# Layer 2's last layer norm in each pair of items applied in the scan layout, and one item's last statistics moved to ScalarE

## The chip, the cores and the metric

The kernel runs on one core of a Trainium2 chip. The metric is the device time of one execution in microseconds (us); lower is better. A core has TensorE (PE, with its weight loads shown as PEld), VectorE (DVE), ScalarE (ACT), GpSimd (POOL) and SyncE (SP, which here only issues DMAs). Each engine works through its own list of instructions in order, and waits for the others by semaphores.

## What is computed

The reference, cut to what matters here (the feed-forward part that follows is not touched by the change):

```python
def _mingru(x, Wz, bz, Wh, bh):
    z = sigmoid(einsum('bsi,hi->bsh', x, Wz) + bz)
    h_tilde = tanh(einsum('bsi,hi->bsh', x, Wh) + bh)
    a = clip(1.0 - z, CLAMP_LO, CLAMP_HI)
    return _linear_scan(a, z * h_tilde)              # along the sequence

def _stack(x, Wz, bz, Wh, bh, gamma, beta):          # 4 layers
    h = x
    for i in range(4):
        h_new = _mingru(h, Wz[i], bz[i], Wh[i], bh[i])
        if i > 0:
            h_new = h_new + h
        h = _layernorm(h_new, gamma, beta)
    return h

h_fwd = _stack(layernorm(x), ...)
h_bwd = flip(_stack(flip(layernorm(x)), ...))
x = x + einsum(concat(h_fwd, h_bwd), fusion_W) + fusion_b
x = x + ffn(layernorm(x))                            # 512 -> 2048 -> 512
```

x is 8 x 512 x 512 in float32 (batch, sequence, features). Both directions use the same weights, and the gates' two weight matrices are the same one, so one product per gate serves sigmoid and tanh.

## The kernel before, in words

**Layout.** Products and scans work with features on the 128 partitions and the sequence along the free axis: a state `h` is 4 chunks (`NC_`) of 128 x 512. The scan runs along the free axis. A layer norm is over the features, that is over partitions and chunks, so PE turns the state first: one group of 4 transposes (L316, in `turned`) gives `pt`, 128 positions by all 512 features, in PSUM.

**A layer norm between layers (`norm`).** For each of 4 row tiles: turn (L316); DVE makes mean and variance (`stats`, L171 to L182); POOL makes the inverse root `rs` (L178); ACT writes the normalised row tile `tok` (`normalise`, L188 and L189). When all four are there, 4 groups of 4 transposes (L325, in `back`) turn them back into `pf`, and ACT writes chunk c of `h` with gamma as scale and beta as bias (L331). Tiles `pt` have 2 PSUM banks (`ps_t`), tiles `pf`, `pr`, `py` share 2 (`ps_f`), the products' `u` have 4 (`ps_u`).

**After the last layer (`norm_last`)** only the statistics are made: turn, `stats` with no shift, and `rs` into a column of `rsv`. The mean is folded into the fusion weights; `rsv` is the scale of the fusion's products (L609).

**Order.** The kernel takes the 8 batch items in 4 pairs. Within a pair there are four streams, called items s = (b,0), (b,1), (b+1,0), (b+1,1) (batch, direction). First layer 0 for both batches, then layers 1, 2, 3, in each the four streams one after the other, each with 4 gate products (`layer`, `gates`). So layer 3 of a pair has 16 products. Then the fusion of both batches, mixed with layer 0 of the next pair.

The order in which instructions are issued is written out by `slot`. A slot issues one unit of work (a product of 4 matmuls and its three ACT activations), then what the queues have ready: `turns` and `backs` (norms), `xturns` and `xbacks` (statistics of the next pair's x, of which `scale_x` turns the scales into `pr`; in the last pair, the tokens of the feed-forward part, `py`). Then come the DVE's end of the unit (clamp L485, product L490, scan L494), then delayed stages of kind "resid", then the ACT part of what was taken from the queues. So on ACT, what a slot turned is drained after that slot's three activations:

```python
last = shares(cap) + x_shares()
due("scans")
if end is not None:
    end()
due("resid")
for f in last:
    if f is not None:
        f()
now[0] += 1
```

In layer 3 the residual sums h + z (L571) of a stream are "resid" stages, chunk c in slot 3 + c counted from the stream's first slot; its turns (`norm_last`) start in slot `now + NC_ + 1`, so that the turns of stream (b,1) come with the first slot of (b+1,1), the thirteenth of the layer. While streams (b+1,0) and (b+1,1) run, the statistics of the next pair's x are made too (L171, `st_x`).

The norm of layer 2's last stream (b+1,1) falls into the first slots of layer 3; its result is needed in the thirteenth.

## Time and profile before

| | |
|---|---|
| median of 3 runs | 1713.87 us (1713.86 to 1713.90) |
| the profiled execution's own time | 1714.24 us |
| its span, first to last instruction | 1712.0 us |
| granted TensorE clock | 1.00 |
| gate products (L462), 1536 matmul instructions | 593 ns mean of one, pipelined |
| turn for a norm (L316), 128 x 128 | 1024 transposes, 273 ns mean, pipelined |
| turn back (L325), 128 x 128 | 768 transposes, 273 ns mean, pipelined |
| scan (L494), 128 x 512 | 256, 1.23 to 1.24 us |
| DVE statistics of a turned tile (L171) | 256, 693 ns |
| DVE sum of two 128 x 512 (L571, L565) | 665 to 693 ns |
| ACT affine from PSUM (L331) | 192, 786 ns |

The span is cut by the profile into PE, DVE, ACT and POOL busy times. A matmul's duration in the profile includes its way through the pipeline, so that the mean of one is longer than the distance between two starts. Idle time before an instruction is given with the engine and line that ended it.

### The profile page before, as it was taken

To read this page: it belongs to the slowest core of one execution; us is meant where nothing else is said; L and a number is where in the kernel's file an instruction comes from. 1 tells how busy PE (TensorE), PEld (TensorE's weight loads), DVE (VectorE), ACT (ScalarE), POOL (GpSimd) and SP (SyncE) were. 2 spreads that over 40 slices of the span, in tenths; PEclk is the share of its full clock that TensorE was granted. 3 is DMA by queue.
4 is the path that set the end of the run, shared out by engine and by line. 5 is a ranking of instruction groups with operands and counts; after the bars stand their busy time and mean duration, and the time that the engine had idled before them with its cause. 6 is when DMAs were issued, how large, how long until landed. Compare 5 with 4: busy or idle time off the path is not lost.

```text
span 1712.0 us, 19766 instructions
## 1 busy us (share of the span) xinstructions
PE 1701.1 (99%) x6440; PEld 1042.4 (61%) x6440; DVE 1453.2 (85%) x2859; ACT 1074.6 (63%) x1858; POOL 222.3 (13%) x342
## 2 busy tenths in 40 slices
PE   9999999999999999999999999999999999999999
PEld 5455554555555455555545555554688888888887
DVE  7999989889998998999899899996568768768877
ACT  5898873468886246888524688860366566666654
POOL 3111111111111111111111111110000000000000
PEclk9999999999999999999999999999999999999999
DMA  8002231150000125000012200202201101100100
GB/s 271 19 25 81 99 93 37 65 193 1 1 19 13 56 68 191 1 1 19 13 56 69 104 21 29 74 1 99 74 1 50 50 0 50 49 19 31 50 19 31
DMA packets 46598, 91.74 MB, mean 54 GB/s; under 512 B 5280, under 2 KB 5536, under 8 KB 45472
## 3 DMA queue, kind: packets, MB, share of 16 engines
q1 hardware_dynamic: 45488, 88.78, 15.3%
q10 hardware_dynamic: 1008, 1.70, 0.3%
q8 instruction: 51, 0.84, 0.2%
q14 instruction: 51, 0.42, 0.1%
HBM read 65.30 MB, written 25.17 MB: 53 GB/s over the span
## 4 chain that ended last, share of the span: by engine, by line
PE 79%; DVE 16%; ACT 2%; issue 1%; DMA 1%; POOL 0%; DVEq 0%; ACTq 0%
PE u L462 28%; PE po L909 14%; PE ph L882 14%; PE pu L599 10%; PE pt L316 5%; DVE z L494 4%; PE pf L325 4%; PE u L511 4%; DVE st L171 2%; DVE z L490 2%; DVE a L485 1%; DVE z L565 1%; DVE zf L494 1%; PE py L214 1%; DVE mv L173 1%
## 5 line engine op out<-in xcount | busy, mean ns | idle before, releaser
L462 PE MATMUL u<-xT,gw 128*128 128x512 f32 x768 | 345.5, 593 | 0.0
L462 PE MATMUL u<-h,gw 128*128 128x512 f32 x768 | 345.5, 592 | 0.0
L494 DVE TENSOR_TENSOR_SCAN z<-a,z 128x512 f32<-128x512 f32 x224 | 274.9, 1227 | 7.6
L462 PEld LDWEIGHTS u<-xT,gw 128*128 128x128 f32 x768 | 138.6, 190 | 138.7 <-issue 136.8
L462 PEld LDWEIGHTS u<-h,gw 128*128 128x128 f32 x768 | 138.6, 190 | 138.2 <-issue 138.0
L479 ACT ACTIVATE a<-u,ngb 128x512 f32<-128x512 f32 x192 | 131.6, 685 | 139.6 <-PE u L462 139.1
L178 POOL TENSOR_TENSOR rs<-ve,mhalf 128x1 f32<-128x1 f32 x192 | 122.3, 637 | 679.8 <-DVE nmu L182 663.2
L171 DVE BATCH_NORM_STATS2 st<-pt 128x6 f32<-128x512 f32 x256 | 177.3, 693 | 37.7 <-PE pt L316 37.3
L909 PE MATMUL po<-pwq,ghi 128*128 128x512 f32 x512 | 202.7, 396 | 0.0
L882 PE MATMUL ph<-yhi,fcq 128*128 128x512 f32 x512 | 199.7, 390 | 0.0
L909 PE MATMUL po<-pwq,glo 128*128 128x512 f32 x512 | 199.6, 390 | 0.0
L882 PE MATMUL ph<-ylo,fcq 128*128 128x512 f32 x512 | 199.4, 389 | 0.0
L886 ACT ACTIVATE g<-ph 128x512 f32<-128x512 f32 x128 | 76.4, 597 | 186.2 <-PE ph L882 186.2
L490 DVE TENSOR_TENSOR z<-z,t 128x512 f32<-128x512 f32 x224 | 153.5, 685 | 10.3 <-ACT z L481 10.1
L189 ACT ACTIVATE tok<-pt,nmr,rs 128x512 f32<-128x512 f32 x192 | 149.3, 778 | 6.4
L897 DVE TENSOR_TENSOR acc<-acc,g 128x512 f32<-128x512 f32 x112 | 77.3, 691 | 84.7 <-ACT g L886 83.8
L481 ACT ACTIVATE z<-u,gb 128x512 f32<-128x512 f32 x192 | 132.4, 689 | 0.0
L480 ACT ACTIVATE t<-u,gb 128x512 f32<-128x512 f32 x192 | 130.8, 681 | 0.0
L316 PEld LDWEIGHTS pt<-ident,z 128*128 128x128 f32 x640 | 78.8, 141 | 77.4 <-issue 47.7
L511 PE MATMUL u<-xT,gw 128*128 128x512 f32 x256 | 115.0, 593 | 1.2 <-DVE gw L744 0.8
L599 PE MATMUL pu<-fw,xT 128*128 128x512 f32 x256 | 115.2, 593 | 0.0
L599 PE MATMUL pu<-fw,h 128*128 128x512 f32 x256 | 115.1, 592 | 0.0
(158 smaller groups left out, 2569.2 us busy)
## 6 DMA issues: line engine op xcount, KB each, us to landing
xf<-in_x_dram SPq DMA_DIRECT2D x32, 256.0 KB, 5.6
x<-xf SPq DMA_DIRECT2D x32, 256.0 KB, 2.0
xy<-x SPq DMA_DIRECT2D x32, 256.0 KB, 4.2
xn<-in_x_dram SPq DMA_DIRECT2D x31, 256.0 KB, 4.5
out_dram<-xy SPq DMA_DIRECT2D x31, 256.0 KB, 2.0
xT<-in_xt_dram SPq DMA_DIRECT2D x7, 1024.0 KB, 7.4
fca<-in_fc_wT_dram SPq DMA_DIRECT2D x16, 256.0 KB, 3.0
pwa<-in_proj_wT_dram SPq DMA_DIRECT2D x16, 256.0 KB, 2.6
```

Source lines behind the costliest of these rows:

```text
L171: nc.vector.bn_stats(st, src)
L189: nc.scalar.activation(dst, src, AF.Identity, bias=nmr, scale=rs)
L316: nc.tensor.transpose(pt[:, ts(c, P)], zs[c][:, ts(t, P)], ident)
L462: nc.tensor.matmul(u, lhsT=gw[l][:, c, ts(o, P)], rhs=h[:, c, :], start=(c == 0), stop=(c == NC_ - 1),)
L479: nc.scalar.activation(a, u, AF.Sigmoid, bias=ngb[:, l, o : o + 1], scale=-1.0)
L481: nc.scalar.activation(z, u, AF.Sigmoid, bias=gb[:, l, o : o + 1])
L490: nc.vector.tensor_tensor(z, z, t, ALU.mult)
L494: nc.vector.tensor_tensor_scan(dst[:, d], a[:, d], z[:, d], 0.0, ALU.mult, ALU.add)
L511: nc.tensor.matmul(u, lhsT=gw[0][:, c, ts(o, P)], rhs=xT[b][:, c, :], start=(c == 0), stop=(c == NC_ - 1),)
L599: nc.tensor.matmul(pu, lhsT=hs[d][:, c, ts(t, P)], rhs=fw[:, d * NC_ + c, :], start=(c == 0), stop=(c == NC_ - 1),)
L882: nc.tensor.matmul(ph, lhsT=w, rhs=ys[b][c][i], start=(c == 0 and i == 0), stop=(c == NC_ - 1 and i == 1),)
L909: nc.tensor.matmul(po[b][t], lhsT=part[:, ts(t, P)], rhs=pwq[k // NP_][:, k % NP_, :], start=(k == 0 and i == 0), stop=(k == NF - 1 and i ...
```

## The change

Two parts, both in the recurrent stage.

1. `norm_flat` replaces `norm` for the last stream (b+1,1) of layer 2 in each pair. The turns and the statistics stay as they are, but the mean and the scale go into the columns of two 128 x 4 tiles (`nmu`, `rs`). No `tok` is written and no token is turned back. Instead PE turns the columns, broadcast to 128 x 128, into two tiles of 128 x 512 in which every partition holds the whole sequence's values (`pf_rs`, `pf_nmu`, 4 transposes each); ACT copies both to SBUF (`nmu` first, then `rs`). Then, in four slots one after the other, DVE adds the first and multiplies by the second to a chunk as it lies, and one slot later ACT applies gamma and beta to that chunk in place. The state is a new tile.
2. `by_scalar` replaces the DVE statistics in `norm_last` for stream (b+1,0). ACT makes them in two passes over the turned tile in PSUM: a copy with a running sum, the negative mean, and a square with the mean as bias and a running sum; DVE makes one 128 x 1 scale and add, POOL the inverse root. The two passes are those that `second` used before for some tiles of x (now shared as `two_passes`).

```diff
-    def stats(src, name, rs=None, shift=True):
+    def stats(src, name, rs=None, shift=True, nmu=None):
...
-        nmu = small.tile([P, 1], F32, tag="nmu", name=f"nmu_{name}")
+        if nmu is None:
+            nmu = small.tile([P, 1], F32, tag="nmu", name=f"nmu_{name}")
...
-                queue(turns, s, now[0] + NC_ + 1, t, tokens(turned(zs, t, f"{tag}_{t}"), None, rsv[s][:, t : t + 1], f"{tag}_{t}"))
+                source, name = turned(zs, t, f"{tag}_{t}"), f"{tag}_{t}"
+                queue(turns, s, now[0] + NC_ + 1, t, by_scalar(s, t, source, name) if s[0] % 2 and s[1] == 0 else
+                      tokens(source, None, rsv[s][:, t : t + 1], name))
+
+        def by_scalar(s, t, source, name):
+            def go():
+                src = source()
+                left[s] += 1
+                def last():
+                    end = two_passes(src, src, rsv[s][:, t : t + 1], name)
+                    def rest():
+                        end()
+                        left[s] -= 1
+                    stages.append((now[0] + 1, "late", rest))
+                return last
+            return go
+
+        def norm_flat(s, zs, tag, pause):
+            toks, at = Tokens(), now[0] + pause
+            cols = {k: small.tile([P, NT], F32, tag=f"flat_{k}", name=f"{k}_{tag}") for k in ("rs", "nmu")}
+            spread = {}
+
+            def statistics(t):
+                def go():
+                    src = turned(zs, t, f"{tag}_{t}")()
+                    stats(src, f"{tag}_{t}", cols["rs"][:, t : t + 1], nmu=cols["nmu"][:, t : t + 1])
+                    return lambda: toks.append(t)
+                return go
+
+            def apply(c):
+                h = state[s][:, c, :]
+                nc.vector.tensor_tensor(h, zs[c], spread["nmu"], ALU.add)
+                nc.vector.tensor_tensor(h, h, spread["rs"], ALU.mult)
+                zlive[0] -= 1
+                def last():
+                    nc.scalar.activation(
+                        h, h, AF.Identity, bias=bet[:, c : c + 1], scale=gam[:, c : c + 1],
+                    )
+                    left[s] -= 1
+                    if c == NC_ - 1:
+                        held[0] -= 2
+                stages.append((now[0] + 1, "late", last))
+
+            def over():
+                state[s] = hp.tile([P, NC_, S], F32, tag="h", name=f"h_{s[0]}{s[1]}")
+                held[0] += 2
+                banks = {}
+                for k, v in cols.items():
+                    banks[k] = ps_f.tile([P, S], F32, tag="pf", name=f"pf_{k}_{tag}")
+                    for t in range(NT):
+                        nc.tensor.transpose(banks[k][:, ts(t, P)], v[:, t : t + 1].broadcast_to([P, P]), ident)
+                left[s] += NC_
+                for c in range(NC_):
+                    stages.append((now[0] + 1 + c, "resid", lambda c=c: apply(c)))
+                def last():
+                    for k in ("nmu", "rs"):
+                        spread[k] = tokp.tile([P, S], F32, tag="tok", name=f"{k}s_{tag}")
+                        nc.scalar.copy(spread[k], banks[k])
+                return last
+
+            for t in range(NT):
+                queue(turns, s, at, t, statistics(t))
+            queue(backs, s, toks, 0, over)
...
+        def two_passes(src, dst, rs, name):
+            sm, nm, ss, ve = (small.tile([P, 1], F32, tag=k, name=f"{k}_{name}") for k in ("sm", "nm", "ss", "ve"))
+            nc.scalar.activation(dst, src, AF.Copy, accum_out=sm)
+            nc.scalar.activation(nm, sm, AF.Copy, scale=-1.0 / H)
+            nc.scalar.activation(dst, src, AF.Square, bias=nm, accum_out=ss)
+            def end():
+                nc.vector.tensor_scalar(ve, ss, 1.0 / H, LN_EPS, ALU.mult, ALU.add)
+                nc.gpsimd.tensor_tensor(rs, ve, mhalf, ALU.pow)
+            return end
...
-            if l < L - 1:
+            if l == L - 2 and s[0] % 2 and s[1] == 1:
+                norm_flat(s, zs, f"{s[0]}{s[1]}_{l}", 2)
+            elif l < L - 1:
                 norm(s, zs, f"{s[0]}{s[1]}_{l}", 2)
```

In the built programs the lists of PE, DVE, ACT and POOL differ in these instructions alone, for pairs 1 to 3 at the same places; in the last pair the last turn for the norm of (b+1,1) and the first `py` come one slot earlier. SP's list is the same. Per pair: PE 16 transposes (L325) out, 8 in. DVE 4 bn_stats and 4 bn_aggr out, 8 tensor_tensor of 128 x 512 in. ACT 4 `nmr` and 4 `tok` out; 2 copies of 128 x 512 and 4 times the two passes in; the four affine activations read SBUF where they read PSUM.

More of the change, by code (lines that the diff above doesn't have):

```diff
@@ L373, in scale_x @@
             return go
+        def two_passes(src, dst, rs, name):
[7 more added lines that the diff above has]
+            return end
         def second(b, t):
             def go():
-                src, name = xs["n", b, t], f"x{b}_{t}"
-                sm, nm, ss, ve = (small.tile([P, 1], F32, tag=k, name=f"{k}_{name}") for k in ("sm", "nm", "ss", "ve"))
-                nc.scalar.activation(src, src, AF.Copy, accum_out=sm)
-                nc.scalar.activation(nm, sm, AF.Copy, scale=-1.0 / H)
-                nc.scalar.activation(src, src, AF.Square, bias=nm, accum_out=ss)
-                def end():
-                    nc.vector.tensor_scalar(ve, ss, 1.0 / H, LN_EPS, ALU.mult, ALU.add)
-                    nc.gpsimd.tensor_tensor(rx[b][:, t : t + 1], ve, mhalf, ALU.pow)
+                src = xs["n", b, t]
+                end = two_passes(src, src, rx[b][:, t : t + 1], f"x{b}_{t}")
                 stages.append((now[0] + 1, "late", end))
```

## The prediction

> **What bounds the kernel now.** I read the page's busy times first, then the PE, DVE and ACT timelines of the stretch that the change edits. All times below are microseconds from the span's start; a timeline row is start, duration, engine, line, operation, tiles, count, and in brackets the idle time before it.

> ```profile
> span 1712.0 us, 19766 instructions
> PE 1701.1 (99%) x6440; PEld 1042.4 (61%) x6440; DVE 1453.2 (85%) x2859; ACT 1074.6 (63%) x1858; POOL 222.3 (13%) x342
> ```

> Busy time of PE is modelled, so I checked it by the distance of starts. I number the sixteen gate products of layer 3 of a pair 0 to 15; T5 is the end of product 5. The second pair (items 2 and 3), product 5's end to product 13's start:

> ```profile
> 521.22 0.79 PE L325 MATMUL pf<-ident,tok 128*128 128x128 f32 x4
> 521.84 0.60 PE L367 MATMUL pr<-ident,rx 128*128 128x128 f32 x4
> 522.27 3.60 PE L462 MATMUL u<-h,gw 128*128 128x512 f32 x8
> 525.71 0.60 PE L325 MATMUL pf<-ident,tok 128*128 128x128 f32 x4
> ...
> 545.95 3.60 PE L462 MATMUL u<-h,gw 128*128 128x512 f32 x8
> 549.38 0.60 PE L316 MATMUL pt<-ident,h 128*128 128x128 f32 x4
> 549.82 3.60 PE L462 MATMUL u<-h,gw 128*128 128x512 f32 x8
> ```

> Eight matmuls take 525.71-522.27 = 3.44, four transposes 526.15-525.71 = 0.44 (0.109 each), and product follows product with no gap: here PE is the bound, and what it does not issue is time saved. The waits in PE's own list add up to some 7 us in all. DVE in the same stretch:

> ```profile
> 531.66 0.69 DVE L490 TENSOR_TENSOR z<-z,t 128x512 f32<-128x512 f32 x1 [0.73 <-ACT z L481]
> 532.39 1.22 DVE L494 TENSOR_TENSOR_SCAN z<-a,z 128x512 f32<-128x512 f32 x1
> 533.53 0.67 DVE L571 TENSOR_TENSOR h<-z,h 128x512 f32<-128x512 f32 x1
> 534.11 0.69 DVE L171 BATCH_NORM_STATS2 st<-pt 128x6 f32<-128x512 f32 x1
> ...
> 543.99 0.69 DVE L171 BATCH_NORM_STATS2 st<-pt 128x6 f32<-128x512 f32 x1
> ...
> 548.35 0.67 DVE L571 TENSOR_TENSOR h<-z,h 128x512 f32<-128x512 f32 x1
> 548.93 0.69 DVE L171 BATCH_NORM_STATS2 st<-pt 128x6 f32<-128x512 f32 x1
> ```

> Up to product 7 DVE idles about 0.9 a product (0.73 of it before L490, for ACT). From product 8 on it has no gap: a product costs it 4.94 (543.99 to 548.93), because it also makes one last-layer and one x statistic, while PE needs 3.87. So DVE falls back 1.07 a product. Now the row to see: the sum h<-z,h at 548.35 ends at 549.02, and it is the last chunk that the transposes pt<-ident,h at 549.38 read. **The cover between DVE and PE is 0.36 us there.** In the first and third pair it is 0.37 and 0.36 (sum ends 250.65 and 847.29, transposes 251.02 and 847.65). In the last pair, without x statistics, it is 3.1:

> ```profile
> 1144.17 0.67 DVE L571 TENSOR_TENSOR h<-z,h 128x512 f32<-128x512 f32 x1
> ```

> against transposes at 1147.97. The chain of waits says the same: between 532 and 580 it runs through DVE alone. ACT in the same product 5:

> ```profile
> 521.52 0.68 ACT L479 ACTIVATE a<-u,ngb 128x512 f32<-128x512 f32 x1
> 522.09 0.69 ACT L480 ACTIVATE t<-u,gb 128x512 f32<-128x512 f32 x1
> 522.66 0.70 ACT L481 ACTIVATE z<-u,gb 128x512 f32<-128x512 f32 x1
> 523.23 0.80 ACT L331 ACTIVATE h<-pf,bet,gam 128x512 f32<-128x512 f32 x1
> 523.89 0.61 ACT L371 COPY scale<-pr 128x512 f32<-128x512 f32 x1
> ```

> What PE turns in a product is drained by ACT only after the three gate activations: the fourth instruction starts 1.71 to 1.73 after the first.

> **The change, part by part.**

> *PE work.* Per pair 16 transposes of tokens (L325) go and 8 of the columns come: 4 pairs x 8 x 0.109 = 3.49 saved, all on PE's path. [...]

> *A wait on a PSUM bank.* ps_f has two banks. Before, product 5 was followed by pf and pr: two tiles. Now the same place issues pf_rs, pf_nmu and then pr, three tiles in a row (py in the last pair). In the built program pr takes the bank of pf_nmu, so it waits for ACT's copy nmus, the fourth ACT instruction of that product: ACT starts a 0.20 after the end of a product (525.71 to 525.91), the copy 1.73 later, takes 0.60 (L371), and PE resumes about 0.10 after such an end: T5+2.63 = 523.85. Without the wait it would come at T5+0.87. Wait: 1.76. Queued behind it on PE is product 6 and all that follows. Bounds: 0, if a bank were free, and 2.23, if the second copy had to end too (0.47 more, the step from L371 at 226.14 to the next ACT start 226.61). I take 1.76, since that bank is what the program names. Product 6 then starts at 523.85+0.44 = 524.29, 2.02 late.

> *The two DVE passes.* Per chunk two 128x512 tensor_tensor, in products 6, 7, 8, 9, behind the scan. Nearest rows: L565 0.69, L571 0.67, both SBUF to SBUF. Start to start they cost 0.72 where the next reads the result (L490 to L494) and 0.59 where not (L571 to L171): 1.31 a chunk. Bounds 1.18 and 1.44. [...]

> Now DVE's time, second pair, from product 6's L490, which follows ACT and so PE: 527.79+2.02 = 529.81. Product 6: 0.72+1.14+0.59+1.31 = 3.76, to 533.57. Product 7: clamp 0.33 and the same, 4.09, to 537.66; the old 0.9 of idle is used up, so no slack takes anything. Products 8 and 9: 4.94+1.31 = 6.25 each, to 550.16. Product 10: its sum starts 4.36 on, 554.52, and ends at 555.19. PE reaches pt<-ident,h at 549.38+2.02-3x0.44 = 550.08 and must hold its fourth transpose to 555.24, 4.8 us; product 13 starts at 555.35 instead of 549.82: **5.5 us late**. First and third pair have the same rows: 5.5 each.

> Last pair: product 4 now has one set of transposes more, so T5 = 1113.79+0.87+3.44 = 1118.10; py at 1120.73, product 6 from 1121.17 to 1124.61, L490 2.08 later (1125.85 to 1127.93) at 1126.69. DVE: 4.36 (with ylo, 0.6), 4.69, 5.78, 5.18 to 1146.70; product 10's sum 3.28 on, ending 1150.65. Product 13 starts at 1150.81 against 1148.41: 2.4 late. Its older wait of PE (0.5 before py at 1126.81) is inside this sum.

> What follows is not late again: after product 12 DVE lags 0.64 more against PE than before (555.19-549.02-5.53), and the next buffers have covers of 3 us (pt has two banks; L171 at 553.87 frees what PE takes at 557.56).

> *Off the path.* ACT loses four nmr (0.30) and tok (0.78) per pair; the four affine activations stay, from SBUF. Each stands behind the DVE pass and holds ACT's queue, the next a, t, z among it: the last ends near 550.5, product 12 reads it from about 549.2 and so ends near 551.5, which the hold to 555.2 covers; uncovered it would cost 1.4 a pair. POOL, SP and the DMAs issue the same lists.

> *Last statistics on ACT.* Four tiles a pair: 0.61+0.19+0.20+0.72+0.19, about 1.9 each (L380 to L382), into waits of ACT of 12.6, 11.5 and 8.3 us in that stretch (576 to 602); without this cover 7.7 a pair. DVE is spared 1.09-0.15 each, 3.8 a pair. It can buy only PE's small waits behind it, where the next pair's transposes wait for a token: 0.16, 0.28 (614.61-610.89-3.44) and 0.63. I credit 1.1; bounds 0 and 2.

> **Sum:** 3x5.53+2.40-1.1 = +17.9. On the profiled execution's own 1714.24 that is 1732.1; the median of the runs is 0.37 lower: **1732**. Its own bounds: DVE passes at 1.18 and 1.44 (4 chunks, 4 pairs: -2.1, +2.1), the second copy (+1.9), the credit (-0.9, +1.1): 1729 to 1737.

> **Rivals.**
> 1. *No bank wait, DVE alone*: if pr found a bank, product 6 would be 0.26 late instead of 2.02 and the sums 1.76 earlier: 3x3.77+0.6-1.1 = +10.8, 1725. For: DVE's part needs nothing from the wait. Against: three tiles, two banks.
> 2. *Bank wait alone*: DVE hides its passes. 3x0.70+0.28-1.1 = +1.3, 1715. For: 15% idle on DVE overall. Against: no gap from product 8 to 15.
> 3. *Faster*: PE's list decides, both holds hidden: 3.49 + the old waits gone (3x0.13+0.52) + 1.1 = 5.5 saved, 1708. For: PE 99%, ACT spared. It decides from the point where DVE's pair of passes costs under 0.1 a chunk on the path, which the cover of 0.36 forbids.
> 4. *ACT's hold adds*: the affine activations waiting on DVE delay the next gates so that DVE waits in turn: 1.4x4 = 5.6 more, 1738.

> **How the numbers follow.** Forecast 0.64, rival 1 0.14, rival 2 0.05, rival 3 0.08, rival 4 and worse 0.09. A measurement here tells 0.2% (3.4 us) from no change: slower 0.64+0.14+0.09 = 0.87, same 0.05, faster 0.08. The range from 1723, under rival 1, to 1739, over rival 4, leaves out rivals 2, 3 and what is worse than 4.

> **What would show it.** In the profile after: PE's wait before pr of about 1.8 once a pair (L367), and one of 4 to 5 before pt<-ident,h, released by DVE, in three pairs, 1.5 to 2.5 in the last; DVE 8 us busier in all (32x0.69-16x(0.69+0.18)); PE with 32 transposes less and, in the fusion, fewer waits for tokens. No wait at pt<-ident,h would make the prediction wrong; so would a pr that starts on time.

## The result, and the profile after

The changed kernel takes 1739.48 us (median; 1739.18 to 1741.36) against 1713.88: a ratio of 1.0151 with a 95% interval of [1.0136, 1.0166], 25.6 us slower. The forecast was 1732 with a range from 1723 to 1739. The direction and most of the mechanism were right; the time lies 7.5 us above the forecast and 0.5 above its range.

The page's span and busy times (the profiled execution took 1739.18):

```profile
span 1737.3 us, 19728 instructions
...
PE 1705.9 (98%) x6408; PEld 1041.3 (60%) x6408; DVE 1459.2 (84%) x2859; ACT 1089.4 (63%) x1914; POOL 222.9 (13%) x342
```

TensorE has the 32 instructions fewer, VectorE is busy 6.0 us longer. The span grew by 25.3, so the cost is in waiting or in slower instructions, and TensorE's list of waits names the first (columns: total, times, longest):

```profile
PE pt L317 <- DVE h L645: 11.7, 4, 3.2
PE pr L437 <- ACT nmus L423: 4.6, 3, 1.5
PE u L536 <- ACT h L400: 3.7, 3, 1.2
...
PE py L215 <- ACT nmus L423: 1.5, 1, 1.5
```

These four lines come to 21.5; the kernel before had none of them. TensorE's timeline in the second pair shows where each stands (L536 is the gate product, L462 before; L317 turns, L645 the residual sum, L571 before):

```profile
529.13 0.60 PE L415 MATMUL pf_rs<-ident,rs 128*128 128x128 f32 x4
529.57 0.60 PE L415 MATMUL pf_nmu<-ident,nmu 128*128 128x128 f32 x4
531.71 0.65 PE L437 MATMUL pr<-ident,rx 128*128 128x128 f32 x4 [1.54 <-ACT nmus L423]
...
558.50 1.13 PE L536 MATMUL u<-h,gw 128*128 128x512 f32 x2 [1.21 <-ACT h L400]
...
563.20 0.47 PE L317 MATMUL pt<-ident,h 128*128 128x128 f32 x1 [3.24 <-DVE h L645]
563.46 6.31 PE L536 MATMUL u<-h,gw 128*128 128x512 f32 x8
```

Product 5 ends at 529.13. The third tile in a row, pr, waits for the bank; product 12 waits for the affine of h; the fourth transpose of h waits for VectorE's sum. Then comes a row that the forecast has no term for: **product 13 lasts 6.31 where eight such matmuls last 3.60**, and it waits for nothing. The windows of the same stretch give the reason (columns: window, length, busy time of PE, PEld, DVE, ACT, POOL with counts, granted TensorE clock, DMA share, GB/s):

```profile
563.20:564.20 1.00, 1.00 (x2) 0.60 (x3) 0.86 (x4) 0.00 (x0) 0.00 (x0) 0.50 0.00 0
...
568.20:569.20 1.00, 1.00 (x3) 0.35 (x2) 0.86 (x4) 0.00 (x0) 0.00 (x0) 0.64 0.00 0
569.20:570.20 1.00, 1.00 (x8) 0.71 (x7) 0.96 (x3) 0.39 (x1) 0.60 (x1) 1.00 0.00 0
```

At the end of the wait the granted clock is 0.50, and it stays there for some 5.7 us (the second window, at 0.64, is at half clock for 0.72 of its 1.00 us, to 568.92); then it is 1.00 again. The busy column alone would have hidden this: a matmul at half clock counts as busy for twice as long (0.85 from start to start in product 13, against 0.43).

VectorE, in products 9 and 10 of that pair, is as forecast (scan, two passes, sum; then the sum of product 10):

```profile
555.07 1.22 DVE L568 TENSOR_TENSOR_SCAN z<-a,z 128x512 f32<-128x512 f32 x1
556.22 0.67 DVE L395 TENSOR_TENSOR h<-z,nmus 128x512 f32<-128x512 f32 x1
556.91 0.69 DVE L396 TENSOR_TENSOR h<-h,rss 128x512 f32<-128x512 f32 x1
557.52 0.68 DVE L645 TENSOR_TENSOR h<-z,h 128x512 f32<-128x512 f32 x1
...
562.48 0.67 DVE L645 TENSOR_TENSOR h<-z,h 128x512 f32<-128x512 f32 x1
```

The passes take 557.52 - 556.22 = 1.30 a chunk, a product costs VectorE 6.26 (its z<-z,t start at 554.36 and 560.62), and the sum ends at 563.15, 0.05 before the transpose that waited for it.

**The ledger.** Measured as distance between starts beyond the usual one, over the whole trace: bank wait 4 x 1.70 = 6.8; affine 3 x 1.39, and 0.10 with each, 4.5; sum 3 x 3.40 + 2.14 = 12.3; lowered clock 6.8. The last is product 13's eight matmuls at 5.76, 6.15 and 4.76 from its first start to the next tile's in the three pairs, against 3.44, and 0.16 on each held transpose. Gone are 1.5 of small waits (0.5 before py, 0.4 among the transposes of the last pf, 0.6 before the next pair's transposes) and 32 x 0.109 = 3.5 of transposes. Sum: 6.8 + 4.5 + 12.3 + 6.8 - 1.5 - 3.5 = 25.4; the span grew by 25.3.

### The profile page after: what moved, and what is told of

It reads as the page before. It is cut to its first block, busy times and chain, and to the rows that moved or that the text cites. A ratio compares the mean times of both kernels' runs of the same rounds, so it can differ in the third digit from the quotient of the medians.

```text
span 1737.3 us, 19728 instructions
## 1 busy us (share of the span) xinstructions
PE 1705.9 (98%) x6408; PEld 1041.3 (60%) x6408; DVE 1459.2 (84%) x2859; ACT 1089.4 (63%) x1914; POOL 222.9 (13%) x342
## 4 chain that ended last, share of the span: by engine, by line
PE 84%; DVE 12%; ACT 2%; issue 1%; DMA 1%; POOL 0%; DVEq 0%; ACTq 0%
PE u L536 27%; PE po L985 13%; PE ph L958 13%; PE pu L675 13%; PE u L585 6%; PE pt L317 5%; PE pf L326 4%; DVE z L568 3%; DVE z L564 2%; DVE st L171 2%; DVE z L639 1%; DVE a L559 1%; PE py L215 1%; DVE h L396 1%; DVE h L645 1%
## 5 line engine op out<-in xcount | busy, mean ns | idle before, releaser
L536 PE MATMUL u<-h,gw 128*128 128x512 f32 x768 | 352.1, 602 | 3.7 <-ACT h L400 3.7
L536 PE MATMUL u<-xT,gw 128*128 128x512 f32 x768 | 345.5, 593 | 0.0
L536 PEld LDWEIGHTS u<-h,gw 128*128 128x128 f32 x768 | 141.5, 194 | 148.3 <-issue 141.4
L536 PEld LDWEIGHTS u<-xT,gw 128*128 128x128 f32 x768 | 138.9, 190 | 140.1 <-issue 138.2
L171 DVE BATCH_NORM_STATS2 st<-pt 128x6 f32<-128x512 f32 x240 | 166.1, 692 | 33.9 <-PE pt L317 33.9
L190 ACT ACTIVATE tok<-pt,nmr,rs 128x512 f32<-128x512 f32 x176 | 136.9, 778 | 5.9
L317 PEld LDWEIGHTS pt<-ident,z 128*128 128x128 f32 x640 | 78.8, 141 | 77.5 <-issue 47.8
```

The lines of the kernel that those rows point to most:

```text
L171: nc.vector.bn_stats(st, src)
L190: nc.scalar.activation(dst, src, AF.Identity, bias=nmr, scale=rs)
L317: nc.tensor.transpose(pt[:, ts(c, P)], zs[c][:, ts(t, P)], ident)
L536: nc.tensor.matmul(u, lhsT=gw[l][:, c, ts(o, P)], rhs=h[:, c, :], start=(c == 0), stop=(c == NC_ - 1),)
```

## The experiments

Line numbers shift by a few from kernel to kernel; the names stay. "Changed kernel" is the one above.

### Is it the gap that lowers the clock?

```diff
+ if fill:
+     pk = ps_u.tile([P, S], F32, tag="u", name=f"fill_{name}")
  for c in range(NC_):
+     if c == NC_ - 1:
+         for i in range(fill):
+             nc.tensor.matmul(pk, lhsT=gw[1][:, 0, 0:P], rhs=gw[1][:, i % NC_, :], start=(i == 0), stop=(i == fill - 1))
      nc.tensor.transpose(pt[:, ts(c, P)], zs[c][:, ts(t, P)], ident)
...
+ fill = 3 if s[0] % 2 == 0 and s[1] == 1 and t == 0 and s[0] + 2 < B else 0
```

An f32 matmul of the code is two rows of the trace, so the three extra ones show as six.

> The changed kernel with three extra 128x512 matmuls on constant weights, six passes of 0.43 us = 2.6 us, between the third and the fourth transpose pt<-ident,h of product 12 in pairs 1 to 3, into a PSUM tile that nobody reads (extra work, the result stays). They lie inside the 3.4 us in which TensorE waits there. Clock theory (the gap itself makes the granted clock fall to 0.50 for the next 5 us, so that product 13 takes 6.3 us in place of 3.6): the wait for the sum h falls to about 0.7, the granted clock stays 1.00 after it, product 13 takes 3.6, and the time falls by 3 x 2.5 = 7.6 to 1732. Rival A (product 13 is slow for its operands, or since VectorE and ScalarE use memory at the same time): product 13 stays at 6.3 and the time at 1739.5. Rival B (product 13 is quick, but VectorE, which has no idle time there, is the bound behind it): 3.6 for product 13, but a new wait of about 2.5 within the next ten products, and 1739.

Measured: 1734.29 us (1733.47 to 1734.42), ratio to the kernel before 1.0117 [1.0101, 1.0132]. TensorE's timeline at the same place:

```profile
557.43 2.74 PE L321 MATMUL fill<-gw 128*128 128x512 f32 x6
560.84 0.33 PE L322 MATMUL pt<-ident,h 128*128 128x128 f32 x1 [0.67 <-DVE h L651]
561.00 3.60 PE L542 MATMUL u<-h,gw 128*128 128x512 f32 x8
564.44 0.60 PE L322 MATMUL pt<-ident,h 128*128 128x128 f32 x4
```

The held transpose still comes 4.70 after the held matmuls of product 12, as in the changed kernel, but product 13 is at full speed, 3.44 from start to start, in all three pairs. So the operands and the other engines are not what slowed it (rival A), and no new wait appears behind it (rival B). The span of the profiled execution is 6.5 shorter, 1730.8 against 1737.3, against the ledger's 6.8. The median fell only 5.2, not 7.6: the expectation had taken 2.5 for each pair where the three stretches differ, and its executions have 1.8 to 3.4 us outside the span (the changed kernel's 1.8 to 1.9), for which there is no row. Two of its four executions also have spans of 1732.5 and 1732.6 at a mean clock of 0.999; that the clock fell once in them is likely, but they left no rows.

### Which half of the change costs?

The first edit leaves the norm alone in place, the second the ScalarE statistics alone.

```diff
- ... by_scalar(s, t, source, name) if s[0] % 2 and s[1] == 0 else
+ ... by_scalar(s, t, source, name) if False else          # first: the norm alone
...
- if l == L - 2 and s[0] % 2 and s[1] == 1:
+ if False:                                                # second: the statistics alone
      norm_flat(s, zs, f"{s[0]}{s[1]}_{l}", 2)
```

> The change's new norm alone: layer 3's statistics of the last item are made on VectorE as before. Theory (all of the loss stands in products 5 to 13, the ScalarE statistics are worth the small token waits behind them, about 0.5): 1740, with the same waits at pr, u and pt<-ident,h as the changed kernel. Rival (the eleven or so ScalarE instructions that a pair gained in the fusion stretch hold up its queue and cost a part of the 25.6): below 1735.

> The ScalarE statistics alone: layer 2's norm is the old one everywhere. Theory: small token waits behind the fusion go, 1713.3 (0.5 below the kernel before; with the credit as forecast 1712.8). Rival (ScalarE's queue is held up in the fusion stretch): above 1717, with new waits of TensorE for ScalarE behind 576 us.

Measured: the norm alone 1740.14 (1.0152 [1.0138, 1.0165]), with the same four lines in TensorE's list of waits; the ScalarE statistics alone 1713.60 (0.9997 [0.9988, 1.0006]). The whole loss is the norm's, as expected. The statistics are worth about half a microsecond by the spans (1711.5 against 1712.0) and by TensorE's waits for tokens (2.1 against 2.6); the times alone don't tell that from no change.

### The bank wait alone

```diff
  def over():
+     crowd[0] = now[0]
...
- return [take(q) for q in (xturns, xbacks) if q and ready(q[0][0])]
+ return [take(q) for q in (xturns, xbacks)
+         if q and ready(q[0][0]) and not (q is xbacks and crowd[0] == now[0])]
...
+ crowd = [-9]
```

> The changed kernel with pr (py in the last pair) taken one product later than the two column tiles, so that it no longer stands third in line for two PSUM banks; nothing else moves. Theory (bank wait and VectorE's lateness add, and the lowered clock follows from the 3.4 us hold, which stays): the wait before pr goes, products 6 to 12 come 1.7 earlier, the hold before the fourth pt<-ident,h stays at 3.4 and product 13 at 6.3; 1739.5 - 4 x 1.7 = 1732.7. Rival (VectorE alone sets the end, the bank wait lies in its shadow): the hold grows by 1.7 and the time stays at 1739.

Measured: 1731.37 (1729.93 to 1732.38), ratio 1.0100 [1.0087, 1.0114]. The two lines of waits for nmus are gone; the wait for the sum is still 3.24 in three pairs, and product 13 still lasts up to 6.5. So the terms add, as the forecast had it: VectorE's lateness does not hide the bank wait. The profiled span is 6.8 shorter, which is 4 x 1.70, but that it is so exact is chance: the wait for the affine shrank too (0.94 in place of 1.39 in three pairs), the last pair's wait for the sum grew from 2.14 to 2.65, and the lowered clock cost some 1.2 more. The spans of the four executions run from 1728.1 to 1730.5.

### The passes off VectorE

Both kernels have pr one product later too; the second also has the passes one product earlier (its edit is in the next section).

```diff
- nc.vector.tensor_tensor(h, zs[c], spread["nmu"], ALU.add)
- nc.vector.tensor_tensor(h, h, spread["rs"], ALU.mult)
+ nc.gpsimd.tensor_tensor(h, zs[c], spread["nmu"], ALU.add)
+ nc.gpsimd.tensor_tensor(h, h, spread["rs"], ALU.mult)
```

> The kernel with pr one product later, and its eight 128x512 passes of a pair (add nmus, multiply by rss) on GpSimd in place of VectorE. Theory (VectorE's lateness makes the holds; without it TensorE keeps its 3.49 us of transposes and some 1 us of small waits): no hold before the fourth pt<-ident,h, granted clock 1.00 there, 1709 to 1711, below the kernel before. Rival (GpSimd's passes are slow, or slow VectorE down by sharing its way to SBUF: VectorE's 128x512 rows, now 0.67 to 0.69, grow, or the pass takes over 2 us and the affine h<-h,bet,gam comes late for product 12): a hold of several us stays, 1720 or more.

> Both: pr one product later, passes on GpSimd, and one product earlier. Theory: as with GpSimd alone, 1709 to 1711, since nothing waits for the passes by then. Rival (the pass on GpSimd costs VectorE as much as making it itself): within 3 us of the early passes on VectorE.

Measured: 1735.79 (1.0126 [1.0112, 1.0140]) and 1734.89 (1.0119 [1.0103, 1.0134]). The theory fell in both. The first kernel's rival holds: a hold of several us stays, and VectorE's rows grow. The second kernel's rival does not: it put the time within 3 us of the early passes on VectorE (1721.00, next section), and it came 13.9 above them. By the rows below, a pair of passes on GpSimd costs VectorE more than making it itself, and the clock fell in three pairs of both profiled executions (mean 0.993 and 0.996). GpSimd's and VectorE's timelines of the second kernel, same stretch:

```profile
530.98 1.30 POOL L395 TENSOR_TENSOR h<-z,nmus 128x512 f32<-128x512 f32 x1 [3.33 <-ACT nmus L424]
532.35 2.07 POOL L396 TENSOR_TENSOR h<-h,rss 128x512 f32<-128x512 f32 x1
```

```profile
531.19 2.17 DVE L572 TENSOR_TENSOR_SCAN z<-a,z 128x512 f32<-128x512 f32 x1
533.28 1.69 DVE L649 TENSOR_TENSOR xT<-z,xT 128x512 f32<-128x512 f32 x1
```

The product before, with GpSimd idle, has 1.23 for the same scan and 0.67 for the same sum; beside the passes they take 2.17 and 1.69. Each is longer by about 1 us: VectorE pays about 2 us for a pair of GpSimd passes where its own pair costs 1.30. The wait for the sum h is 3.8 at most here. The scan ends 1.08 after GpSimd's first pass has ended (533.36 - 532.28), close to its whole length of 1.23, and the sum 0.55 after the second (534.97 - 534.42), close to its 0.67: as if most of each had run only behind the pass. What holds them there, a shared way to SBUF, as the first kernel's rival had it, or something else, no row shows.

### The passes one product earlier

```diff
- for c in range(NC_):
-     stages.append((now[0] + 1 + c, "resid", lambda c=c: apply(c)))
+ for c in range(1, NC_):
+     stages.append((now[0] + c, "resid", lambda c=c: apply(c)))
...
      nc.scalar.copy(spread[k], banks[k])
+ apply(0)                                                          # right behind the two copies
```

> The kernel with pr one product later, and the four pairs of passes on VectorE one product earlier (products 5 to 8 in place of 6 to 9), where VectorE still idles. Theory: one pair of passes, 1.31 us, leaves the stretch in which VectorE has no idle time; the two holds of TensorE, together 0.94 + 3.40 before, make 3.0 in pairs 1 to 3 and 1.3 in the last, 1731.4 - 5.2 = 1726.2 if the granted clock still falls after a gap of 3.0, and near 1719 if it needs more than that. Rival (the early pass stands in front of product 6's clamp and holds up ScalarE and TensorE in turn): a new wait in products 6 and 7, 1730 or more.

Measured (with pr late): 1721.00 (1719.30 to 1723.95), ratio 1.0040 [1.0028, 1.0053]. The wait for the affine is gone, the one for the sum is 3.1, 3.1 and 3.4 from start to start (3.0 expected) and 1.0 in the last pair (1.3 expected). The time lies between the two that were expected with and without a fall of the clock. In the profiled execution product 13 lasts 3.60 behind each of them: the clock stayed at 1.00. The mean clock of the five timed executions runs from 0.997 to 1.000, and the slowest clock has the longest time; that the clock fell in some of them is likely, but they left no rows.

### The statistics that stand in VectorE's way

VectorE's products 8 to 11 hold one x statistic each for the next pair. They were moved eight products later, or to ScalarE (the tile pr that needs them then comes later too):

```diff
- norm_x(s[0] + 2, now[0])
+ norm_x(s[0] + 2, now[0] + 8 * (s[0] % 2))                            # later
+ norm_x(s[0] + 2, now[0], (0, 1, 2, 3) if s[0] % 2 else ())           # or on ScalarE
```

> pr one product later, passes on VectorE one product earlier, and the x statistics of the next pair's second item, which stood in products 8 to 11, made eight products later, in the fusion. Theory (the hold of 3.1 to 3.4 that is left before the fourth pt<-ident,h is VectorE's work in products 8 to 10, three x statistics of 1.09 each among it): no hold in pairs 1 to 3, 1.0 in the last, which has no x statistics; the granted clock stays 1.00; 1721.0 less 3 x 3.1 and the clock's share of some 1.5: 1710, below the kernel before. Rival (VectorE has no room in the fusion either: TensorE waits there for up to 4.4 a pair): 1715 to 1722, with new waits of TensorE behind 577 us.

> The changed kernel with only the x statistics of products 8 to 11 made eight products later; bank wait and the place of the passes as changed. Theory: the sum h comes 3 x 1.09 = 3.3 earlier, of the two holds of 1.4 and 3.4 some 1.5 are left, no gap is over 3, the granted clock stays 1.00: 1739.5 - 3 x 3.3 - 6.8 = 1723. Rival (the clock falls for another reason than the gap): 1730, with product 13 still over 5 us. Rival (VectorE has no room in the fusion): over 1727 with new waits there.

> The kernel before with the same x statistics made eight products later: what that move is worth by itself. Theory: TensorE is the bound in products 8 to 13 there, nothing is won; in the fusion VectorE has four statistics more a pair than before: between 1713.5 and 1717. If it wins over 2 us, a gain of the kernel with all three edits isn't the change's.

Measured: with pr late and the passes early 1714.42 (1.0002 [0.9993, 1.0011]); in the changed kernel alone 1728.00 (1.0081 [1.0068, 1.0095]); in the kernel before 1721.45 (1.0046 [1.0034, 1.0059]). The part of the theory on products 8 to 13 holds: no hold in pairs 1 to 3 of the first kernel, 1.67 in place of 1.39 + 3.40 in the second. The part on the rest does not (1714.42 in place of 1710, and 1721.45 in place of at most 1717): VectorE has no room in the fusion, and TensorE waits there for xf (up to 2.4 in the kernel before, up to 0.9 in the first) and for tokens. The second kernel missed its 1723 by these waits, and because its clock fell at a place where I had not expected it, in the last pair; that is taken up below.

> pr one product later, passes one product earlier, and the same four x statistics of a pair made on ScalarE, where they stood (two passes of 0.6 to 0.7 a tile and two small ones). Theory: VectorE is spared 3 x 0.94 = 2.8 before the sum; the hold falls to 0.3, 1712. Rival (ScalarE, with three gate activations of 1.72, the affine of 0.72 and 1.71 for the statistics a product, 4.15 against TensorE's 3.87, comes late with a, t, z, and VectorE waits for it): a hold of 2 or more stays, 1717 or more.

> The kernel before with the x statistics of products 8 to 11 made on ScalarE: the control for the kernel that came out below the kernel before. Theory (that gain is the change's own: 32 transposes of 0.109 and the small waits that its ScalarE statistics take away): TensorE is the bound here too and its list is the old one, 1713.5 to 1714.2. Rival (the gain is that of the moved x statistics): 1710 to 1711.

Measured: 1709.91 (1709.80 to 1710.27), ratio **0.9976 [0.9966, 0.9985]**, and for the control, the same statistics on ScalarE in the kernel before, 1713.75 (0.9998 [0.9989, 1.0007]). TensorE's timeline of the first, between products 12 and 13 and at product 13:

```profile
547.42 0.67 PE L317 MATMUL pt<-ident,h 128*128 128x128 f32 x4
547.92 3.60 PE L540 MATMUL u<-h,gw 128*128 128x512 f32 x8
```

547.42 to 547.92 is 0.50 for four transposes that usually take 0.44: the hold is 0.06. The rival was not far off: ScalarE's instructions stand close together from 539.3 to 550.4, but its gates still come in time. The 1712 expected was 2 too high mostly because it started from a median, 1721.0, in which a fallen clock was still contained; the executions at clock 1.000 took 1719.3. The gain of some 4 us belongs to the change: 3.5 of transposes, 1.4 of small waits gone, less 1.0 of hold in the last pair, is 3.9, and the span is 3.9 shorter (1708.1 against 1712.0). Moving the statistics alone, in the control, brings less than can be told from no change. Of the other two edits, one moves passes that only the change has, and the other takes away a wait before pr that the kernel before doesn't have.

### From which gap on does the clock fall?

The runs so far contradict any single length. Two rows, the last pair of the changed kernel and the last pair of the changed kernel with later x statistics:

```profile
1173.58 0.33 PE L317 MATMUL pt<-ident,h 128*128 128x128 f32 x1 [1.98 <-DVE h L645]
1173.74 3.60 PE L536 MATMUL u<-h,gw 128*128 128x512 f32 x8
```

```profile
1161.36 0.33 PE L317 MATMUL pt<-ident,h 128*128 128x128 f32 x1 [1.98 <-DVE h L645]
1161.52 5.29 PE L536 MATMUL u<-h,gw 128*128 128x512 f32 x8
```

The same place, the same idle time of 1.98, full clock in the first and half clock in the second. So gaps of known lengths were put ahead of the kernel before, 54 bursts of matmuls with a chain of VectorE instructions between them:

```diff
...
+ for r in range(3):
+     for k in range(1, 10):
+         for m in range(2):
+             pk = ps_u.tile([P, S], F32, tag="u", name=f"busy_{r}_{k}_{m}")
+             n = 12 + (r + k + m) % 3
+             for i in range(n):
+                 nc.tensor.matmul(pk, lhsT=ones if i else gapw[:, 0:P], rhs=dat, start=(i == 0), stop=(i == n - 1))
+             nc.vector.tensor_scalar(gapw[:, 0:P], pk[:, 0:P], 0.0, None, ALU.mult)
+             for w in [512] * k + [128] * m:
+                 nc.vector.tensor_scalar(gapw[:, 0:w], gapw[:, 0:w], 1.0, None, ALU.mult)
```

> The kernel before with a measured piece ahead of it (extra work): 54 bursts of 12 to 14 matmuls of constants, 10 to 12 us each at full clock, and between two bursts TensorE waits for a chain of VectorE instructions of 0.5 to some 4.5 us; its time means nothing, its rows do. Theory A (a gap lowers the clock once it is longer than some fixed length): a sharp edge between 2.1 and 3.4 us, no slow burst below, every burst slow above. Theory B (the clock is judged over stretches of time that don't start with the gap, so that the same gap lowers it or not by where it falls): from 2.1 to about 3.4 some bursts slow and some not, for gaps of the same length, and the slow part of a burst between 3 and 7 us long.

The program took 2541.46 us with this piece in it (one execution). Two stretches of TensorE's timeline, each with the end of a gap of 2.12 in it:

```profile
83.69 1.45 PE L245 MATMUL busy<-dat,gapw 128*128 128x512 f32 x2 [2.12 <-DVE gapw L248]
84.93 11.85 PE L245 MATMUL busy<-dat,ones 128*128 128x512 f32 x24
```

```profile
361.73 1.10 PE L245 MATMUL busy<-dat,gapw 128*128 128x512 f32 x2 [2.12 <-DVE gapw L248]
362.67 11.32 PE L245 MATMUL busy<-dat,ones 128*128 128x512 f32 x26
```

The rows of a burst's first matmul are in its first line. The first burst runs slow at its start: its other 24 rows take longer than the 26 of the second. Over all 53 gaps, by idle time (start to start less the 0.59 that a matmul row of this piece covers):

```
idle before the burst     bursts   with half clock at their start
0.85 to 1.86 us             15        0
2.12 to 3.25 us             18        8
3.51 to 4.89 us             20       20
```

Theory B holds. A slow burst is 1.5 to 2.9 longer than its count of matmuls takes at full clock, mostly 1.7: four rows of 0.85 in place of 0.43, a stretch of 3.4. The edge is a band, and within it the same gap can go either way. What differs, by the traces, is where a gap lies against the places at which the clock changes. In the changed kernel it falls at 254.90, 562.10, 869.30 and, at the end, 1736.28, and is back at 261.72, 568.92 and 872.71. The shortest stretch at half clock, 869.30 to 872.71, is 3.413 long, like the slow stretch of mostly 3.4 above, and all seven changes lie whole multiples of 3.4133 apart, to within 0.01: from 254.90 to 562.10 it is 307.20 = 90 x 3.4133, and after these two falls the clock is back two such lengths later:

```profile
254.80:254.90 0.10, 0.00 (x0) 0.00 (x0) 0.08 (x1) 0.10 (x3) 0.00 (x0) 0.98 0.38 143
254.90:255.00 0.10, 0.00 (x0) 0.00 (x0) 0.09 (x1) 0.10 (x2) 0.00 (x0) 0.50 0.28 103
...
562.00:562.10 0.10, 0.00 (x0) 0.00 (x0) 0.10 (x1) 0.10 (x2) 0.00 (x0) 0.97 0.00 0
562.10:562.20 0.10, 0.00 (x0) 0.00 (x0) 0.10 (x1) 0.10 (x1) 0.00 (x0) 0.50 0.00 0
```

With the trace of the gaps cut into stretches of 3.413 at the changes of its own clock, the 53 gaps part by how much of one stretch they fill (a gap counted from 0.43 after the start of the last row before it). Of 27 gaps that filled at least 0.62 of a stretch, all lowered the clock; of 24 that filled at most 0.57, none did; of two between, at 0.58 and 0.59, the one at 0.58 did. So in this trace the clock fell behind a stretch of which about 0.6, some 2.0 us, was idle: an estimate from these 53 gaps, since no run set the place of a gap on purpose. The changed kernel agrees, by the same count with 0.11 for a transpose: the stretches right before its falls at 254.90, 562.10 and 869.30 are idle for 0.65, 0.70 and 0.85 of their length, and none of the others at full clock, between the first and the last of the trace, for more than 0.51. The two rows of 1.98 fit. In the second a stretch begins at 1158.48, one length before the fall at 1161.89, and holds the whole wait; in the first one begins at 1173.08, 88 lengths after the change at 872.71, and cuts the wait in two. Two waits in one stretch can make up the share together: before the fall at 254.90 the stretch held 0.6 of the wait for the affine and 1.5 of that for the sum. By the same estimate a gap would lower the clock for certain only from twice 2.0, some 4.1 us, on; that all nine gaps of 3.51 to 3.97 did so is in part luck.

## Why the prediction was right or wrong

- *PE work, 3.49 saved*: right, 32 instructions fewer at 0.109. The kernel that removes the holds in pairs 1 to 3 shows the gain.
- *A wait on a PSUM bank, 1.76 a pair*: 1.70 measured, in all four pairs, behind the copy that was named; TensorE resumed 0.06 after that copy's end (531.71 against 531.06 + 0.59), where the forecast put about 0.10. Taking it away made the span 6.8 shorter, so rival 1 (no such wait) and rival 2 (nothing else) are out.
- *The two DVE passes, 1.31 a chunk*: 1.30 measured. A product of 6.25 was forecast, 6.26 came. The hold was forecast at 4.8 from the time TensorE would have been there; 1.39 + 3.40 = 4.79 came. Against the end of product 5, product 13 is later by (563.46 - 529.13) - (549.82 - 521.22) = 5.73, of which 0.16 is the clock; 5.53 was forecast. VectorE became 6.0 busier, not the 8 that was given as a sign: that sum counts whole rows, which overlap by up to 0.1 (556.91 + 0.69 against 557.52: 0.08); by distance of starts it is 16 x (1.30 - 0.94) = 5.8.
- *ACT's hold, 1.4 and covered*: right, it is the first 1.39 of that 4.79. Rival 4, which had it come on top, is out; its 1738 lay near the result for another reason.
- *Last statistics on ACT, hidden; credit 1.1*: hidden, but the small waits gone behind the fusion were 0.12 and 0.47, so the credit was 0.5 too high.
- **The step that failed** is "What follows is not late again" behind the hold: the sum went on at full clock after an idle time of TensorE that it put itself at 4.8 in three pairs. There is no term for the granted clock, and the page of before, where the clock has hardly a dip, gave no row to find it by. The runs showed half clock there: product 13 took 4.76 to 6.15 from start to start against 3.44, and again 3.44 once matmuls filled the gap. It cost 6.8 of the 7.4 between the sum (17.9) and the growth of the span (25.3); the credit is most of the rest. Without the clock the forecast's own steps come to 18.6 as measured.
- The range was too narrow for the same reason: its upper end was worked out from bounds on the known terms and from rival 4, and none of them let an instruction that does not wait take longer.

## What to carry to other kernels

An instruction saved on the bounding engine is worth its time only if the work that replaces it fits the other engines at that very place: here eight VectorE passes a pair, a wait for a PSUM bank and the clock that fell behind the passes' wait turned 3.5 us of gain into 25 of loss, and the same change gains 4 once the third PSUM tile is moved a product on, the passes stand where VectorE idles, and four statistics go to ScalarE. Of the gaps put in, 8 of 18 of 2.12 to 3.25 us, and all 20 of 3.51 to 4.89, were followed by half clock for some 3 to 6 us: a forecast that makes TensorE wait that long needs a second term for it, at a chance that is read from such counts. And a pass that VectorE has no room for is not free on GpSimd: a pair there made VectorE's scan and sum 0.94 and 1.02 longer, where VectorE's own pair costs 1.30.
